# A three-part decoder layer on one core: the scores of all sixteen heads of a batch in one burst, and buffers by planned slot

## The chip, the cores and the metric

The kernel runs on one core of a Trainium2 chip. The metric is the device time of one execution in microseconds; lower is better. Engine names follow the profile: PE (TensorE, matrix products), PEld (its weight loads), DVE (VectorE), ACT (ScalarE), POOL (GpSimd), SP (SyncE, which issues DMAs).

## The reference

One pre-norm decoder layer on x of shape 8 x 112 x 512 in float32:

```python
x = x + attn(layernorm(x))            # 16 heads of 32, RoPE on q and k, causal, biases on q, k, v and the output
x = x + xattn(layernorm(x), ctx)      # q from x; k and v from ctx (375 x 128) by one expansion; causal over (query, key)
x = x + ffn(layernorm(x))             # fp8 products: gelu(x Wg0) * (x Wg1), then Wlin; hidden size 2048
```

Softmax is over the keys, `scores / sqrt(32)`. In cross-attention the causal mask lets query t see context rows 0 to t only, so only 112 of the 375 context rows take part. Each of the two attentions is thus, for each batch and head, a 112 x 112 score matrix with a head size of 32.

## The kernel before

The kernel is written as operations on a planner. `plan.op(eng, cost, fn, r, w, ...)` records one operation with its engine (or a choice of two), an estimated cost, and the buffers that it reads and writes. `Plan.order()` then simulates the engines once, in Python, and fixes the order in which every engine's instructions are issued; on the chip each engine runs its own list in that order and waits on semaphores. Nothing is decided on the chip. Priorities are a longest path (`rank`) and a due time (`plan.at` with the offsets `OFF`, weighted by `BETA`); `SLACK` says how far apart two start times may lie and still be ranked by priority. `CAPS` limits how many buffers of each role are in use.

Tokens: 896 = 7 tiles of 128 (`NT`), but attention works on batches of S = 112. Activations that feed products are held transposed, features on partitions, as a high and a low part (`fm`), and the projections are three products each (`mm3`, line 418: high x high, high x low, low x high).

The steps that matter here:

- `rope_evac` (lines 450 to 462): ACT takes q or k out of PSUM with its bias (`qr`), two SP DMAs swap neighbours (`qs`), DVE or POOL multiply by cos and sin (459, 460) and add (462) into `q` or `k`. It is done by group of four batches (`QG`) and by chunk `m` of four heads.
- `values` (lines 537, 539): v is projected by token tile into `vt` and moved by SP DMAs into `v_sb`, by batch.
- `attention(kind, b)`: for each batch, heads come in four chunks `c` of four heads. Scores (line 479) are taken in bursts of `PAIR` chunks: a head is a 32-row operand, and the four heads of a chunk use the four 32-row tiles of the array at once (mode "row"). Row tile r writes PSUM bank `banks[r]`, so that a burst takes four banks of role `s` (`CAPS["s"]` is 4), and chunk j of the burst takes columns j*112 to (j+1)*112. In the trace each float32 score product is two matmul records.
- For each chunk and head: DVE scales, masks and takes the minimum of the negated scores (line 489, tile `P`), ACT takes the exponential with its sum (492). For each chunk DVE takes the reciprocal (495), POOL or DVE multiplies (496), PE transposes the four 112 x 112 blocks (503, bank `pt`), and ACT or DVE copies them to `pts` (382).
- AV (line 513), when all four chunks are ready: 16 heads, each writing 32 columns of the array (mode "col"), into bank `av`; ACT and DVE split it into `fm` (386, 387).
- `out_proj` (418, 526), `layernorm` (370 to 375, 402 or 400), `cross_kv`, `cross_q`, and `ffn` (646, 653 to 656, 670, 676).

The planner charges a cost `ENTER` when PE changes between ordinary products ("full"), row tiles and column tiles; before the change the transposes count as "full".

Buffers: all eight PSUM banks are one pool with one tag, and all twelve 512-wide temporaries in SBUF (`tmp`: weight staging, `xn`, `qr`, `qs`, `vt`, `P`, `pts` and others) are one tag `t` with twelve buffers. The plan counts how many are free, by role. Which physical buffer a new tile gets is decided by turn in the order of allocation: the one that was allocated longest ago. The tile framework makes the first writer wait until that buffer's last reader is done.

## Time and profile before

| | |
|---|---|
| median of 3 runs | 301.65 us (300.61 to 302.99) |
| the profiled execution | 301.63 us, of which 299.8 us from the first to the last instruction (the span) |
| mean granted TensorE clock | 0.993 |
| score records (line 479) | 512, in 32 bursts of 16; PE busy 22.8 us |
| transposes of P (line 503) | 256; PE busy 36.0 us |
| AV records (line 513) | 512, in 16 bursts of 32; PE busy 15.8 us |
| DVE mask and minimum (line 489) | 256; busy 53.8 us, mean 267 ns |
| ACT exponential (line 492) | 256; busy 96.4 us, mean 382 ns, and 49.2 us of reading the sums, which overlap the next one |

How to read it: busy time of an engine is the union of its instructions. Neighbouring matmuls overlap in the records, since their ends are modelled; the time that one holds PE is read from its start to the start of the next. Self-attention lies between 41 us (first scores) and 142 us (last AV at 140.8), cross-attention between 152 and 226, and from there to 296 only the feed-forward part is left.

### The profile page before, as it was taken

How to read it: one execution, taken by the hardware profiler on the slowest of the kernel's cores; microseconds unless marked ns; L12 is line 12 of the kernel's file. 1: busy time of each engine (PE TensorE's matmuls, PEld its weight loads, DVE VectorE, ACT ScalarE, POOL GpSimd, SP SyncE). 2: the span in 40 equal slices, each digit the busy share in tenths (PEclk: the TensorE clock that was granted, in tenths of full speed). 3: DMA queues.
4: the chain of work that ended last, by engine and by line, in shares of the span. 5: the costliest groups of instructions: out<-in, count | busy, mean ns of one | idle time of the engine just before them, and what ended most of it. 6: DMA issues, size and time to landing. Idle time of an engine off the chain costs nothing.

```text
span 299.8 us, 7577 instructions
## 1 busy us (share of the span) xinstructions
PE 285.9 (95%) x2656; PEld 227.9 (76%) x2656; DVE 228.9 (76%) x909; ACT 203.4 (68%) x710; POOL 108.8 (36%) x111
## 2 busy tenths in 40 slices
PE   7799999896999999999999999999999999999995
PEld 2589877695677777778999987778787577776884
DVE  3798899596599899979559889999967546544564
ACT  4444564358389799999079989999857546545552
POOL 4881518915406478345411442353310101010010
PEclk9999999999899999999999999999999999999999
DMA  7955550301023412207999400000000001010011
GB/s 227 319 176 174 199 192 32 128 32 62 33 68 108 136 43 73 66 3 72 109 104 103 41 2 1 3 2 3 1 2 0 3 0 72 0 37 36 2 72 35
DMA packets 14790, 20.78 MB, mean 69 GB/s; under 512 B 3232, under 2 KB 7584, under 8 KB 14752
## 3 DMA queue, kind: packets, MB, share of 16 engines
q1 hardware_dynamic: 11632, 17.15, 17.5%
q0 software_dynamic: 3120, 3.15, 11.4%
q8 instruction: 21, 0.34, 0.5%
q14 instruction: 17, 0.14, 0.2%
HBM read 22.39 MB, written 1.84 MB: 81 GB/s over the span
## 4 chain that ended last, share of the span: by engine, by line
PE 63%; DVE 3%; ACT 2%; POOL 0%; issue 0%
PE psm L418 22%; PE psfg L646 16%; PE psfo L670 8%; PE pspt L503 7%; PE pss L479 4%; PE psav L513 4%; ACT P L492 1%; PE psm L402 1%; DVE P L489 1%; PE psm L400 1%; DVE pts L382 1%; DVE xnx L375 1%; POOL wxqwl L346 0%; DVE P L496 0%; DVE vt L537 0%
## 5 line engine op out<-in xcount | busy, mean ns | idle before, releaser
L492 ACT ACTIVATE P<-P,at 112x112 f32<-112x112 f32 x256 | 96.4, 382 | 17.4 <-DVE at L489 17.3
L489 DVE CUSTOM_DVE_ANT_0 P<-pss,mask 112x112 f32<-112x112 f32 x256 | 53.8, 267 | 10.4 <-POOL k L462 3.2
L496 POOL TENSOR_TENSOR P<-P,at 112x448 f32<-112x448 f32 x41 | 39.5, 963 | 57.9 <-DVE at L495 29.9
L492 ACT ACTIVATION_READ_ACCUMULATOR P<-P,at 112x1 f32 x256 | 49.2, 192 | 0.0
L503 PE MATMUL pspt<-ident,P 112*112 112x112 f32 x256 | 36.0, 263 | 0.3 <-DVE P L496 0.3
L503 PEld LDWEIGHTS pspt<-ident,P 112*112 112x112 f32 x256 | 27.3, 133 | 8.4 <-issue 2.2
L646 PE MATMUL psfg<-x,wgwh 128*128 128x256 fp8e4 (+1 forms) x256 | 29.1, 259 | 0.0
L646 PE MATMUL psfg<-x,wgwl 128*128 128x256 fp8e4 (+1 forms) x256 | 29.1, 259 | 0.0
L655 DVE TENSOR_TENSOR fb<-gb,fb 128x512 bf16<-128x512 bf16 x28 | 11.5, 421 | 19.1 <-ACT fb L382 17.0
L382 ACT COPY pts<-pspt 112x448 f32<-112x448 f32 x36 | 19.1, 529 | 10.1 <-PE pspt L503 6.3
L646 PEld LDWEIGHTS <-wgwl 128*128 128x128 fp8e4 x256 | 22.4, 98 | 4.4 <-issue 0.3
L479 PE MATMUL pss<-k,q 32*112 32x112 f32 x512 | 22.8, 285 | 2.1 <-DVE at L489 1.4
L646 PEld LDWEIGHTS <-wgwh 128*128 128x128 fp8e4 x256 | 22.2, 98 | 2.9 <-issue 0.7
L479 PEld LDWEIGHTS pss<-k,q 32*112 32x112 f32 x512 | 16.8, 175 | 9.3 <-DVE at L489 2.5
L676 POOL TENSOR_TENSOR x_sb<-x_sb,ob 128x512 f32<-128x512 f32 x3 | 3.5, 1154 | 51.4 <-ACT ob L382 51.4
L489 DVE DVE_READ_ACCUMULATOR2_ANT at<- 112x1 f32 x256 | 21.0, 82 | 0.0
L382 DVE COPY pts<-pspt 112x448 f32<-112x448 f32 x28 | 17.3, 616 | 2.9 <-POOL wxqwl L346 1.3
L565 POOL TENSOR_TENSOR x_sb<-x_sb,bo_t 128x512 f32<-128x512 f32 x7 | 14.5, 2089 | 9.8 <-DMA bo_t<-in_bo_dram 9.8
L653 ACT ACTIVATE gb<-gb 128x512 bf16<-128x512 bf16 x28 | 17.2, 633 | 0.5
L386 ACT CAST fmh<-psm 128x512 fp32r<-128x512 f32 x14 | 8.0, 587 | 12.8 <-PE psm L402 12.8
L496 DVE TENSOR_TENSOR P<-P,at 112x448 f32<-112x448 f32 x23 | 16.1, 705 | 0.4
L382 ACT CAST fb<-psfg 128x512 bf16<-128x512 f32 x14 | 8.3, 590 | 11.9 <-PE psfg L646 11.6
(138 smaller groups left out, 721.8 us busy)
## 6 DMA issues: line engine op xcount, KB each, us to landing
qs<-qr SPq DMA_DIRECT2D x32, 112.0 KB, 2.0
x_sb<-in_x_dram SPq DMA_DIRECT2D x7, 256.0 KB, 4.4
out_dram<-x_sb SPq DMA_DIRECT2D x6, 256.0 KB, 2.0
wst<-in_Wv_dram SPq DMA_DIRECT2D x4, 256.0 KB, 4.3
wst<-in_Wq_dram SPq DMA_DIRECT2D x4, 256.0 KB, 3.5
wst<-in_Wk_dram SPq DMA_DIRECT2D x4, 256.0 KB, 4.2
wst<-in_Wo_dram SPq DMA_DIRECT2D x4, 256.0 KB, 3.2
wst<-in_xWqT_dram SPq DMA_DIRECT2D x4, 256.0 KB, 3.0
```

Source lines behind the costliest of these rows:

```text
L382: lambda e: A.copy(dst(), src()) if e == "act" else V.tensor_copy(dst(), src()), r=r, w=w)
L418: T.matmul(out=out(), lhsT=l(a), rhs=r(b), start=(j == 0 and q == 0), stop=(j == tot - 1 and q == 2))
L479: T.matmul(out=banks[r]()[:S, j * S : (j + 1) * S], lhsT=qk[0]()[rs, c, t0 : t0 + S], rhs=qk[1]()[rs, c, t0 : t0 + S], start=True, stop=True)
L489: op("dve", 0.194, lambda ps=ps, r=r, j=j, Pv=Pv, sm=sm: V.tensor_tensor_reduce(Pv()[:, r, :], ps()[:S, j * S : (j + 1) * S], mask(), -SCA ...
L492: op("act", 0.373, lambda r=r, Pv=Pv, sm=sm: A.activation(Pv()[:, r, :], Pv()[:, r, :], AF.Exp, bias=sm()[:S, r : r + 1], scale=-1.0, accu ...
L496: op(("pool", "dve"), (0.935, 0.535), lambda e, sm=sm, Pv=Pv: LO[e][0].tensor_tensor(Pv(), Pv(), sm()[:S, 8:12].unsqueeze(2).broadcast_to( ...
L503: T.transpose(pt()[:S, r * S : (r + 1) * S], Pv()[:, r, :], ident()[:S, :S])
L513: T.matmul(out=av()[r * 32 : (r + 1) * 32, c * S : (c + 1) * S], lhsT=v_sb()[:, b, h * 32 : (h + 1) * 32], rhs=pts()[:S, r * S : (r + 1) * ...
L565: op("pool", 1.225, lambda i=i: G.tensor_tensor(x_sb()[:, i, :], x_sb()[:, i, :], bo_t(), ALU.add), r=[bo_t], w=[(x_sb, i)], lock=BOTH)
L646: T.matmul(out=ps()[:, j * n : (j + 1) * n], lhsT=wg()[i][:, c, (m + j) * 128 : (m + j + 1) * 128], rhs=x8()[:, c, t0:t1], start=(c == 0), ...
L653: op("act", 0.105 + w / 1200, lambda gb=gb: A.activation(gb()[:, :w], gb()[:, :w], AF.Gelu_apprx_tanh), w=[gb], tab="gelu")
L670: T.matmul(out=ps()[:, :wd], lhsT=a8()[:, m, s], rhs=wl()[0][:, m, hs], start=(m == 0), stop=(m == NH - 1))
```

## The change

`PAIR` goes from 2 to 4: one burst per batch makes the scores of all sixteen heads, 16 products in 32 records, in the same four banks, now with 4 x 112 of their 512 columns in use. The plan's cost for entering a mode now depends on the mode left as well, and transposes have a mode of their own, "tr". The buffers: the plan remembers for each buffer which slot of its role it took, and each slot becomes a tag of its own with a single buffer, so that a tile gets the slot that the plan picked. The planner's constants (`SLACK`, `BETA`, `PAD`, `PADL`, `OFF`) are others, and a few costs differ; the order on every engine is computed anew from these. No instruction is added to or removed from the kernel's work apart from that: the products, transposes and vector operations are the same in number.

```diff
-PAIR = 2
+PAIR = 4
...
         self.tags, self.make, self.ap, self.turn = tags, make, None, {}
+        self.slot = None
...
-            self.ap = self.make()
+            self.ap = self.make(self.slot)
...
-    ENTER = {"full": 0.17, "row": 0.19, "col": 0.13}
+    ENTER = {
+        "full": {"row": 0.27, "col": 0.27, "tr": 0.02}, "tr": {"row": 0.165, "col": 0.165},
+        "row": {"full": 0.095, "tr": 0.095, "col": 0.165}, "col": {"full": 0.095, "tr": 0.095, "row": 0.165},
+    }
...
-        slots = {t: [(0.0, None)] * c for t, c in self.caps.items()}
+        slots = {t: [(0.0, None, k) for k in range(c)] for t, c in self.caps.items()}
...
                     if e == "pe" and o.mode != mode:
-                        late, at = at + MODE, at + self.ENTER[o.mode]
+                        late, at = at + MODE * ("tr" not in (o.mode, mode)), at + self.ENTER[o.mode].get(mode, 0.0)
                     elif e == "pe" and at > f + 0.05:
                         at += 0.09
                     key = (max(late, f + SLACK.get(e, 0.0)), -(o.rank + o.prio), o.n)
...
                         o.after.append(slots[t][k][1])
+                        b.slot = (b.slot or {}) | {t: slots[t][k][2]}
...
-                        slots[t].append((end + 0.2, o))
+                        slots[t].append((end + 0.2, o, b.slot[t]))
...
-SLACK = {'pool': 0.0, 'dve': 0.016728493955868652, 'pe': 0.0, 'sp': 4.441491789066645, 'act': 0.0667493910742207}
-SWITCH, BETA, PAD, PADL, MODE = 20.0, 7.557163650189596, 1.0312597848408145, 1.1187956159584096, 0.0
+SLACK = {'pool': 1.1509329884673878, 'dve': 0.0, 'pe': 0.14620811115369542, 'sp': 3.3963357599814703, 'act': 0.07133249620527977}
+SWITCH, BETA, PAD, PADL, MODE = 20.0, 12.77588534500499, 1.038936327633465, 1.2783297992029616, 0.0
...
     def bank(role):
-        return Buf(("p", role), lambda: psum.tile([128, 512], F32, tag="p", name=nm("ps" + role)))
+        return Buf(("p", role), lambda k: psum.tile([128, 512], F32, tag=f"p{k['p']}", name=nm("ps" + role), bufs=1))
...
     def tmp(name, dt=F32, extra=()):
-        return Buf(("t", *extra), lambda: sb.tile([128, 512], dt, tag="t", name=nm(name), bufs=CAPS["t"]))
+        return Buf(("t", *extra), lambda k: sb.tile([128, 512], dt, tag=f"t{k['t']}", name=nm(name)))
...
-        op("pool", 0.4, lambda: G.tensor_tensor(c(1), c(0), mhalf(), ALU.pow), r=[sm, mhalf], w=[sm], lock=BOTH)
+        op("pool", 0.5, lambda: G.tensor_tensor(c(1), c(0), mhalf(), ALU.pow), r=[sm, mhalf], w=[sm], lock=BOTH)
...
-            op("pe", 0.187 * PAIR, scores, r=[k for c in cs for d in qk for k in K(d, t0, t0 + S, c)], w=banks,
+            op("pe", 0.19 * PAIR, scores, r=[k for c in cs for d in qk for k in K(d, t0, t0 + S, c)], w=banks,
                cols=224 * PAIR, mode="row")
...
-                op("pe", 0.384 + 0.06, tr, r=[*((P, r) for r in range(4)), ident], w=[pt], cols=448)
+                op("pe", 0.384, tr, r=[*((P, r) for r in range(4)), ident], w=[pt], cols=448, mode="tr")
```

The transposes in `layernorm` get `mode="tr"` too, the small buffers (`half`, `sbuf`) get a tag by slot as `tmp` does, and the offsets in `OFF` all change (for example "qk" from -1322.28 to -1337.29, "a" from -2834.99 to -2582.67, "bo" from 684.86 to 1217.33).

## The prediction, made before the result was known

> **What bounds the kernel now.** I read the page's engine line first, then busy time by stage, then the order on TensorE (PE) at its change points, then the waits.

> ```profile
> PE 285.9 (95%) x2656; PEld 227.9 (76%) x2656; DVE 228.9 (76%) x909; ACT 203.4 (68%) x710; POOL 108.8 (36%) x111
> 41.00:60.00 19.00, 16.60 (x107) 13.71 (x106) 15.06 (x50) 9.67 (x34) 14.93 (x8) 1.00 0.27 94
> 60.00:94.00 34.00, 31.11 (x281) 24.19 (x282) 26.45 (x123) 22.78 (x96) 13.06 (x13) 0.95 0.16 51
> 94.00:142.00 48.00, 46.93 (x527) 36.70 (x528) 44.36 (x220) 45.44 (x188) 26.42 (x28) 1.00 0.32 72
> 142.00:152.00 10.00, 10.00 (x59) 9.39 (x58) 5.32 (x13) 2.45 (x6) 3.49 (x5) 1.00 1.06 108
> 152.00:226.00 74.00, 74.00 (x907) 61.14 (x909) 66.17 (x362) 63.81 (x288) 24.71 (x28) 1.00 0.25 24
> 226.00:296.00 70.00, 70.00 (x620) 53.60 (x608) 39.24 (x88) 39.98 (x70) 5.03 (x5) 1.00 0.07 24
> ```

> The first line is the page's; the others are stretches (columns: length, then busy PE, PEld, DVE, ACT, POOL, then clock, DMA share, GB/s). The reader is to see that from 142 us to the end PE has no gap at all, and from 94 to 142 it lacks 1.1 us. 41 to 94 is different: there PE is idle for 5.3 us and its clock falls to 0.95. While attention runs (94 to 142 and 152 to 226), DVE and ACT are close behind, at 86 to 95%. So time is PE work plus PE's early gaps, with two engines near enough to take over.

> **Part 1: one burst of scores in place of two.** PE's timeline shows what a burst costs in its place:

> ```profile
> 162.24 0.28 PE L418 MATMUL psm<-fmh,wxqwl 128*128 128x256 f32 x1
> 162.45 0.66 PE L479 MATMUL pss<-k,q 32*112 32x112 f32 x16
> 163.04 0.59 PE L503 MATMUL pspt<-ident,P 112*112 112x112 f32 x4
> 163.41 0.36 PE L418 MATMUL psm<-fmh,wxqwh 128*128 128x256 f32 x1
> ...
> 165.56 0.59 PE L503 MATMUL pspt<-ident,P 112*112 112x112 f32 x4
> 166.08 0.66 PE L479 MATMUL pss<-k,q 32*112 32x112 f32 x16
> 166.67 0.39 PE L418 MATMUL psm<-fmh,wxqwh 128*128 128x256 f32 x1
> ```

> Read starts, not durations (ends overlap). A burst holds PE 0.59 us (162.45 to 163.04): four rounds of four records, one per 32-row tile. Narrow windows on the same burst show its rounds beginning at 162.45, 162.65 and 162.74: 0.2 us to get going, then 0.10 per round, and about 0.19 from the last round to the next operation. The neighbours pay too. A projection step of 0.12 us takes 0.21 before a burst (+0.09). Four transposes take 0.317 between projections, 0.365 after a burst (+0.05) and 0.478 before one (+0.16). So a whole burst costs 0.59 + 0.16 + 0.02 = 0.77 between transposes and projection (18 of the 32), 0.73 between projection and transposes, 0.79 between projections. Inside a longer burst, the same eight score products are four more rounds: 0.39. AV, 32 records in one burst at 0.905 us, is the nearest row for a burst of 32; 0.59 + 0.39 = 0.98 agrees within 0.08. Each burst absorbed saves 0.34 to 0.40, say 0.37. There are 8 batches in self- and 8 in cross-attention: 16 x 0.37 = **5.9 us less PE work** (5.4 to 6.3).

> How much of it reaches the end? Twelve of the sixteen lie after 94 us, where PE has no gap to lose it in: 4.4 us. Four lie before that, where the next stall can eat it: 0.7 of 1.5. Taken: **-5.1**.

> [...]

> **Part 2: AV next to the scores.** Now mostly AV, transposes, burst (165.56, above). Directly joined, AV and burst would spare about 0.18 (the transposes' 0.16 back to nothing and the 0.02 behind). The one joined pair in the trace, at 68.16 and 68.75, shows 0.59 and 0.91: the join itself adds nothing. Up to 15 junctions: 0 to -2.7. But MODE is 0.0, and `key`, by which the plan picks PE's next operation, uses `late`, into which only MODE goes; ENTER moves only the plan's own times. So the pairs meet by chance: **-0.7**.

> **Part 3: buffers as picked.** The two large early PE stalls come out of buffer turns:

> ```profile
> 59.85 1.22 PE L479 MATMUL pss<-k,q 32*112 32x112 f32 x16 [1.43 <-DVE at L489]
> 73.22 0.59 PE L418 MATMUL psm<-wvwh,fmh 128*128 128x512 f32 x1 [2.31 <-DVE at L489]
> ...
> 59.51 0.28 DVE L489 CUSTOM_DVE_ANT_0 P<-pss,mask 112x112 f32<-112x112 f32 x1 [3.14 <-DMA v_sb<-vt]
> 72.88 0.27 DVE L489 CUSTOM_DVE_ANT_0 P<-pss,mask 112x112 f32<-112x112 f32 x1 [2.44 <-POOL k L462]
> ```

> DVE's softmax step has its scores, yet waits for a DMA that reads `vt` and for POOL's rope sum: neither makes anything it needs; they were the last readers of the `t` buffer whose turn it was. Behind it the score banks stay full, and PE waits. At 73.22 PE wants a bank for values and gets, by turn, one that still holds scores. Cost: 1.43 + 2.31; then six projections 0.43 apart at half clock instead of 0.23 (+1.2) and the burst at 59.85 lasting 1.15 instead of 0.59 (+0.56): 5.5 us. With the planned slot there is no wait the plan doesn't know of; but the plan may know these, having only 12 slots. Between 0 and -5.5, I take **-2.5**. The new tags and slot bookkeeping issue no instruction.

> **Part 4: what a burst now waits for.** It needs q and k of all four chunks. Now the first burst starts at 41.40 and the second, which needs the other chunks, at 52.45, when DVE ends the last rope sums (50.85 to 52.53). Queued behind the burst on PE is whatever the plan puts there; DVE's 8 softmax steps and ACT's 8 exponentials (of 0.375 start to start) come later with it. DVE's work is only exchanged with rope work; ACT loses up to 3.0 us of early work, in a stage where it is idle 39% of the time. Between 0 and +11.05 (the full delay), I take **+1.5**, the nearest cover being ACT's idle time. In steady running no new wait: a burst still needs all four score banks, and the `P` tiles are still four, so the wait for the oldest `P` still comes one chunk after the banks are free. The new order constants, POOL's 0.5 in place of 0.4 for the layernorm power and the new SLACK only redraw the order; no row prices that, and it widens the range by 3 either way.

> **Sum.** 299.8 - 5.1 - 0.7 - 2.5 + 1.5 = 293.0 span. The profiled execution took 301.63 around it (+1.8), the median is 301.65: **294.8 us**. Less than 1% (3 us) can't be told from no change.

> **Rivals.**

> *Evacuation takes over*: PE's saving turns into PE gaps, DVE and ACT hold the 8.5 us per batch. [...] For it: 95% ACT from 94 to 142. Against: idle ACT time of 7.5 us from 142 to 152, and feed-forward products that already fill PE from 200 on.

> *The late first burst decides* (slower): the exponentials start 11.05 us later. From 94 on, DVE and ACT at 92 to 95% can't catch up, PE runs out of projections (the last of the values now begins near 92) and waits. Then 301.6 + 11.05 - 5.9 = 306.8. It decides once the last AV of self-attention comes over 7 us later than now (140.8). Against: 39% idle ACT time before 94, and a PE that today reaches the cross stage with 10 us of its own work in hand.

> *Larger gain*: all early stalls go and the pairs join: 301.6 - 5.9 - 2.7 - 5.5 = 287.5.

> *The change doesn't do what it says*: the burst stalls inside, since its banks come free and its chunks come ready one by one. The first burst now, which waits inside for a q sum, takes 1.5 us (41.40 to 42.93) in place of 0.59; a wait of 0.37 in each of 16 cancels part 1: about 300. Held within the first rival.

> **How the numbers follow.** Forecast (289.5 to 298.6): 0.52. Evacuation, or stalls inside bursts: 0.13. Late burst or an order as bad: 0.23. Larger gain: 0.12. Faster is the first plus the last: 0.64; same 0.13; slower 0.23. The range drops a tenth on each side: 288 to 305; the forecast's own range is 289.5 to 298.6.

> **What would show it.** L479: 16 bursts of 32 records, each 0.90 to 0.98 us to the next start. PE busy near 279, idle near 13. `P L489` no longer waiting for `vt` or rope sums. DVE and ACT still below PE from 152 to 226. First burst near 50. It is wrong if PE shows new gaps after 94 us, if the last self-attention AV is past 148, or if the burst's start-to-start is over 1.2 us.

## The result, and the profile after

The changed kernel takes 304.77 us (median of 9 runs, 303.21 to 309.23); the kernel before, measured along with it, 302.45. The ratio is 1.0082 (95% interval 1.0053 to 1.0111): a little slower, where 294.8 was forecast. Executions more than 1.5% above the fastest of their kernel are left out of the ratios here and below, but not of the medians. The profiled execution has a span of 302.8 us. Only the mean PE clock tells at once that something has happened: 0.977, against 0.993 before.

Page of the kernel after, span and engine line:

```profile
span 302.8 us, 7575 instructions
PE 285.4 (94%) x2656; PEld 231.1 (76%) x2656; DVE 229.6 (76%) x914; ACT 202.4 (67%) x703; POOL 103.1 (34%) x113
```

PE is busy 285.4 us, hardly less than the 285.9 before; 279 was expected. Its timeline around a burst (line numbers of `attention` are five higher after the change: scores 484, mask 494, transposes 508):

```profile
107.31 0.59 PE L508 MATMUL pspt<-ident,P 112*112 112x112 f32 x4
107.83 1.05 PE L484 MATMUL pss<-k,q 32*112 32x112 f32 x32
108.82 0.50 PE L423 MATMUL psm<-wowh,fmh 128*128 128x512 f32 x1
```

From start to start the burst of 32 holds PE for 0.99 us, in place of two that took 0.59 and their neighbours' extra. There are 16 of these, 13 of them at 0.98 to 0.99; the saving is there. Some stretches show what has swallowed it (columns: from and to, length, busy PE, PEld, DVE, ACT, POOL, clock, DMA share, GB/s):

```profile
41.00:60.00 19.00, 17.27 (x130) 15.11 (x130) 17.14 (x60) 10.05 (x39) 3.36 (x3) 0.91 0.34 117
60.00:94.00 34.00, 30.48 (x290) 23.98 (x289) 26.21 (x125) 24.27 (x104) 15.71 (x15) 0.95 0.18 59
94.00:102.00 8.00, 5.35 (x45) 4.38 (x44) 3.62 (x22) 3.19 (x16) 1.87 (x2) 0.79 0.13 36
102.00:142.00 40.00, 40.00 (x442) 32.75 (x444) 37.93 (x190) 35.84 (x147) 22.70 (x25) 1.00 0.21 61
172.00:185.00 13.00, 11.00 (x106) 8.65 (x105) 9.43 (x54) 9.06 (x42) 6.16 (x7) 0.87 0.68 68
185.00:228.00 43.00, 43.00 (x550) 34.56 (x549) 40.25 (x204) 38.21 (x165) 18.09 (x22) 1.00 0.01 2
```

Wherever PE has gaps in these rows the clock falls too: 0.91, 0.95, 0.79 and 0.87. Stretch by stretch, 1 - clock times the length is 1.7 us. That is four windows of 3.4 us at half clock (granted clock 0.50 from 54.1, 84.8, 98.4 and 180.4 us on, 1.00 in the rest of the span), a loss of up to 6.8 us of PE time, where before there was one (0.51 from 73.4 to 76.9 us). PE's timeline has a gap ahead of each window; in brackets stand its length and what ended it:

```profile
52.83 0.46 PE L484 MATMUL pss<-k,q 32*112 32x112 f32 x8 [1.73 <-DVE k L467]
...
83.57 1.52 PE L484 MATMUL pss<-k,q 32*112 32x112 f32 x32 [1.70 <-DVE at L494]
85.02 0.79 PE L423 MATMUL psm<-wvwh,fmh 128*128 128x512 f32 x1
85.61 0.63 PE L423 MATMUL psm<-wvwl,fmh 128*128 128x512 f32 x1
...
97.97 2.18 PE L484 MATMUL pss<-k,q 32*112 32x112 f32 x30 [2.65 <-DVE at L494]
...
179.47 0.47 PE L423 MATMUL psm<-ch,wkvh 128*128 128x448 f32 x1 [1.26 <-ACT ch L591]
```

In the two gaps near 82 and 95 a burst waits for the masking step, because its banks are still full. The first of these bursts then holds PE 1.45 us instead of 0.98, though the clock is full until 84.8: four masking steps, 0.20 us apart from 83.23 on, free its banks one by one. Behind it, at half clock, the first projection step takes 0.59 us (85.02 to 85.61); behind the burst above it takes 0.34 (108.82 to 109.16). The chain of waits in the window 79 to 101 us goes on from there (start, length, what):

```profile
79.39 0.43 SPq L544
79.87 3.23 DMA v_sb<-vt
83.23 0.28 DVE P L494
83.57 1.52 PE pss L484 x32
...
90.13 2.37 DMA v_sb<-vt
92.62 0.09 DVE vt L542
...
93.90 3.58 DMA v_sb<-vt
97.64 0.27 DVE P L494
97.97 2.18 PE pss L484 x30
```

Masking needs nothing of `vt`. It waits for the DMA that reads `vt` since its `P` tile has been given that memory. The plan's slots put it there: `order()` frees a slot at `end + 0.2`, and for a DMA `end` is when SP has issued it. The plan counts the landing for those who read what the DMA writes, but not for the buffer that it reads. Here SP's issue took 0.43 us and the DMA another 2.4 to 3.6, so for about 3 us `vt`'s slot counts as free in the plan while the DMA is still reading it, and can be picked as the earliest one.

### The profile page after: what moved, and what is told of

It reads as the page before. It is cut to its first block, busy times and chain, and to the rows that moved or that the text cites. A ratio compares the mean times of both kernels' runs of the same rounds, so it can differ in the third digit from the quotient of the medians.

```text
span 302.8 us, 7575 instructions
## 1 busy us (share of the span) xinstructions
PE 285.4 (94%) x2656; PEld 231.1 (76%) x2656; DVE 229.6 (76%) x914; ACT 202.4 (67%) x703; POOL 103.1 (34%) x113
## 4 chain that ended last, share of the span: by engine, by line
PE 80%; DMA 8%; DVE 6%; issue 2%; ACT 1%; SPq 1%; POOL 1%; DVEq 0%; ACTq 0%; POOLq 0%
PE psm L423 37%; PE psfg L651 16%; PE psfo L675 8%; PE pspt L508 8%; PE pss L484 5%; PE psav L518 4%; DMA v_sb<-vt 3%; DMA cst<-in_ctxT_dram 3%; DMA x_sb<-in_x_dram 2%; PE psm L407 2%; DVE P L494 1%; DVE qr L464 1%; SPq L320 1%; DVE pts L387 1%; DMA qs<-qr 1%
## 5 line engine op out<-in xcount | busy, mean ns | idle before, releaser
L501 POOL TENSOR_TENSOR P<-P,at 112x448 f32<-112x448 f32 x48 | 45.1, 944 | 71.7 <-DVE at L500 48.6
L508 PE MATMUL pspt<-ident,P 112*112 112x112 f32 x256 | 37.1, 268 | 0.7 <-ACT pts L387 0.7
L508 PEld LDWEIGHTS pspt<-ident,P 112*112 112x112 f32 x256 | 28.4, 136 | 8.4 <-issue 1.9
L387 DVE COPY pts<-pspt 112x448 f32<-112x448 f32 x35 | 21.7, 620 | 6.7 <-PE pspt L508 6.0
L660 DVE TENSOR_TENSOR fb<-gb,fb 128x512 bf16<-128x512 bf16 x28 | 11.6, 422 | 17.6 <-ACT fb L387 15.3
L484 PE MATMUL pss<-k,q 32*112 32x112 f32 x512 | 19.2, 276 | 6.1 <-DVE at L494 4.4
L387 ACT COPY pts<-pspt 112x448 f32<-112x448 f32 x29 | 15.4, 531 | 7.8 <-PE pspt L508 7.5
L387 ACT CAST fb<-psfg 128x512 bf16<-128x512 f32 x16 | 9.4, 587 | 12.3 <-PE psfg L651 12.1
L518 PE MATMUL psav<-pts,v_sb 112*32 112x112 f32 x512 | 15.6, 262 | 0.8 <-ACT pts L387 0.8
L518 PEld LDWEIGHTS psav<-pts,v_sb 112*32 112x32 f32 x512 | 11.7, 109 | 5.7 <-ACT pts L387 1.6
L423 PE MATMUL psm<-fmh,wxqwh 128*128 128x256 f32 (+1 forms) x48 | 15.3, 319 | 0.0
```

What stands on the lines that cost most here:

```text
L387: lambda e: A.copy(dst(), src()) if e == "act" else V.tensor_copy(dst(), src()), r=r, w=w)
L423: T.matmul(out=out(), lhsT=l(a), rhs=r(b), start=(j == 0 and q == 0), stop=(j == tot - 1 and q == 2))
L484: T.matmul(out=banks[r]()[:S, j * S : (j + 1) * S], lhsT=qk[0]()[rs, c, t0 : t0 + S], rhs=qk[1]()[rs, c, t0 : t0 + S], start=True, stop=True)
L501: op(("pool", "dve"), (0.935, 0.535), lambda e, sm=sm, Pv=Pv: LO[e][0].tensor_tensor(Pv(), Pv(), sm()[:S, 8:12].unsqueeze(2).broadcast_to( ...
L508: T.transpose(pt()[:S, r * S : (r + 1) * S], Pv()[:, r, :], ident()[:S, :S])
L518: T.matmul(out=av()[r * 32 : (r + 1) * 32, c * S : (c + 1) * S], lhsT=v_sb()[:, b, h * 32 : (h + 1) * 32], rhs=pts()[:S, r * S : (r + 1) * ...
```

## The experiments

All of them compute the whole layer. Ratios are to the kernel before, run beside each on the same chip.

| kernel | what it is (`vt` in memory of its own: see a_vtown) | median us | ratio (95%) |
|---|---|---|---|
| after | the change | 304.77 | 1.0082 (1.0053 to 1.0111) |
| a_vtown | after's order, `vt` in memory of its own | 293.27 | 0.9685 (0.966 to 0.971) |
| a_rot | after's order, buffers by turn | 294.54 | 0.9721 (0.9695 to 0.9746) |
| b_slot | before's order, planned slots | 301.3 | 0.993 (0.9903 to 0.9958) |
| a_split | after, each burst split by a mode change | 306.15 | 1.0104 (1.0064 to 1.0145) |
| v_split | a_vtown, each burst split | 297.69 | 0.9818 (0.9771 to 0.9866) |
| b_vtown | b_slot, `vt` in memory of its own | 297.01 | 0.9803 (0.9755 to 0.9851) |
| a_dma | after, slot free at the DMA's landing | 296.17 | 0.9749 (0.9704 to 0.9795) |
| v_pair2 | a_vtown with `PAIR = 2` | 312.36 | 1.0275 (1.0202 to 1.0347) |
| a_warm | after, two gaps filled with products of zeros | 302.21 | 0.9952 (0.9926 to 0.9978) |
| r_vtown | a_rot, `vt` in memory of its own | 296.7 | 0.975 (0.9704 to 0.9795) |
| dv_11 | version with the causes mended | 294.82 | 0.9703 (0.9661 to 0.9745) |
| dv_13 | the same, other constants | 292.63 | 0.9646 (0.9612 to 0.9681) |

**Take away what makes P wait: a_vtown.** The order on every engine stays; the two `vt` tiles move into `a8`, which lies idle until the feed-forward part.

```diff
-        vt = tmp("vt", extra=("vt",))
+        vt = Buf(("t", "vt"), lambda k: a8()[:, k["vt"] * 4 : k["vt"] * 4 + 4, :].bitcast(F32).rearrange("p a b -> p (a b)"))
```

> The kernel after, with its whole issue order unchanged; only the two value tiles vt lie in memory of their own (in a8, idle until the feed-forward part), so that no P tile takes over a buffer that a vt DMA still reads. Theory 1 (P waits for vt's DMA, PE stalls behind it, and its clock halves): the DVE waits of 2.65 and 3.79 us on v_sb<-vt go, with them the PE gaps of 1.7 and 2.65 us near 82 and 95 and one or two of the four half-clock windows (1.7 us each): 297 to 301 us, clock above 0.98. Theory 2 (DVE and ACT set the pace, the saved PE time has nowhere to go): the same 304 to 305. Theory 3 (the new order is worse as such): 303 to 305.

Measured: 0.9685 (293.27 us), faster than theory 1's 297 to 301. Page of a_vtown, span and engine line:

```profile
span 291.2 us, 7559 instructions
PE 277.9 (95%) x2656; PEld 225.0 (77%) x2656; DVE 228.2 (78%) x914; ACT 201.6 (69%) x703; POOL 103.8 (36%) x113
```

Its stretch for the first half of self-attention (columns as above):

```profile
60.00:94.00 34.00, 31.95 (x335) 24.92 (x334) 31.87 (x160) 28.55 (x126) 18.85 (x18) 1.00 0.21 67
```

The clock stays at 1.00, and from 60 to 94 us DVE does 31.87 us of work where it did 26.21. Against the kernel after, the span is 11.6 us shorter: 4.1 of idle PE time (17.4 to 13.3) and 7.5 of busy PE time (285.4 to 277.9), of which the four half-clock windows account for up to 6.8. By this count the two waits on `vt` stand for their two gaps and two of the windows, some 7.8 us (1.70 + 2.65 + 2 x 1.7, an estimate). The other two windows, up to 3.4 us, went as well, and that was not foreseen: the gaps ahead of them are shorter here (1.36 us at 52 and 0.99 at 168). Theories 2 and 3 (DVE and ACT set the pace; the order as such is worse) fall: with the same order and the same evacuation the kernel is 3.2% faster than before.

**Buffers by turn in the new order: a_rot.**

```diff
-        return Buf(("t", *extra), lambda k: sb.tile([128, 512], dt, tag=f"t{k['t']}", name=nm(name)))
+        return Buf(("t", *extra), lambda k: sb.tile([128, 512], dt, tag="t", name=nm(name), bufs=CAPS["t"]))
```

The PSUM banks, `half` and `sbuf` likewise.

> The kernel after with the same order on every engine, but buffers by turn as before the change. The prediction's part 3 (planned slots spare waits): slower by 1 to 5 us, 306 to 310, with more DVE waits at the masking step. Theory 1 (a planned slot hands P the vt buffer whose DMA the plan does not count): within 2 us of 304.8 either way, the vt waits replaced by other ones.

Both theories missed: 0.9721, some 11 us faster than the kernel after (1.0082). The waits of masking in a_rot that are left (us in total, times, longest):

```profile
DVE P L494 <- POOL wxqwl L351: 1.2, 1, 1.2
DVE P L494 <- PE pss L484: 0.7, 2, 0.5
DVE P L494 <- POOL P L501: 0.5, 1, 0.5
DVE P L494 <- PE psav L518: 0.2, 1, 0.2
```

None is on `vt`. By turn, `P` gets the buffer allocated longest ago. The plan picks the one that it believes free first, which can be just the one whose DMA has been issued. So the slots alone cost the kernel after about 3.6% of its time.

**Planned slots in the old order: b_slot.** The reverse edit on the kernel before.

> The kernel before with the same order on every engine, only its buffers by planned slot. The prediction's part 3: 2.5 us faster (0 to 5.5), the DVE waits on v_sb<-vt and on the rope sum at the masking step gone. Theory 1: the plan frees vt's slot at the DMA's issue, so a P tile still lands on it: 0 to 1.5 us faster at most.

Measured 0.993 (0.9903 to 0.9958): about 2 us faster, near the 2.5 of the prediction, but not in the way that was predicted. Its masking waits:

```profile
DVE P L491 <- DMA v_sb<-vt: 6.3, 2, 3.5
DVE P L491 <- PE pss L481: 1.6, 5, 0.7
DVE P L491 <- PE pspt L505: 1.0, 1, 1.0
```

The wait on the rope sum (3.2 us before) is gone, and the one on `vt` has doubled, from 3.1 us before to 6.3.

**Planned slots in the old order, without the DMA wait: b_vtown.** b_slot with the edit of a_vtown.

> The kernel before in its own order, with planned slots and vt in memory of its own: the change's buffers alone, without the wait that they brought. Theory 1: b_slot's two waits on v_sb<-vt (6.3 us of DVE) and its two half-clock windows go, 296 to 299. If the wait matters only in the after order: 301 as b_slot.

As theory 1 said: 0.9803. Page of b_vtown, span and engine line:

```profile
span 294.9 us, 7559 instructions
PE 283.3 (96%) x2656; PEld 226.3 (77%) x2656; DVE 235.0 (80%) x909; ACT 203.2 (69%) x710; POOL 104.7 (36%) x111
```

At nearly full clock (1.000 and 0.997), PE is busy 283.3 us here and 277.9 in a_vtown. The burst and the order together are worth 5.4 us of PE work, and in time the step from 0.9803 to 0.9685, 1.2% or 3.6 us.

**Is PE's work what the time is made of? a_split and v_split.** The burst is split where it was two, by one tiny full-array product into columns that nothing reads:

```diff
                 for j, c in enumerate(cs):
+                    if j == 2:
+                        T.matmul(out=banks[0]()[:, 448:452], lhsT=zero()[:, :128], rhs=zero()[:, :4], start=True, stop=True)
                     for r in range(4):
```

> The kernel after with the same order, but between chunks 1 and 2 of each burst one tiny full-array product (4 columns of zeros, into unused columns of the burst's first bank), so that PE changes its tiling twice more per batch, as two bursts did. The price of a split is about 0.40 us each, 16 of them 6.4 us. Prediction's part 1 (PE work passes to the end): slower by 4 to 7 us, 309 to 312. Theory 2 (DVE and ACT set the pace): slower by less than 1.5 us.

In the kernel after the answer stayed open: 1.0104 against 1.0082, with overlapping intervals, where 309 to 312 us was expected of part 1. PE is busy 288.8 us, 3.4 more, and the span is the same. The clock hides part of the cost: 0.977 to 0.989 over these runs, 0.972 to 0.978 over those of after, and the profile has three half-clock windows in place of four, 1.7 us less lost. So the same was done where there are no such gaps.

> a_vtown (293.3 us, the after order with vt in memory of its own) with the tiny full-array product between chunks 1 and 2 of each burst, in the same order. Without the large stalls PE sets the pace, so the split should now show in full: 16 x 0.40 = 6.4 us, 298 to 300.5. If DVE and ACT set the pace (theory 2), the cost hides: below 295.

```profile
span 295.3 us, 7593 instructions
PE 283.2 (96%) x2672; PEld 228.1 (77%) x2672; DVE 230.6 (78%) x914; ACT 201.8 (68%) x703; POOL 103.2 (35%) x113
```

Page of v_split: PE's busy time grows from 277.9 to 283.2, 0.33 us for each split, and the time by 4.4 us by the medians (297.69 against 293.27), which come from two sessions, or 4.0 by the ratios (0.0133 of 303). That is just under the expected 298 and far from hidden: three quarters or more of PE's added work reach the end.

**One line in the plan: a_dma.**

```diff
-                        slots[t].append((end + 0.2, o, b.slot[t]))
+                        slots[t].append((max(end + 0.2, dma + 0.9 if o.mb else 0.0), o, b.slot[t]))
```

> The kernel after with one line of the plan changed: a buffer that a DMA reads comes free when the DMA is expected to land, not 0.2 us after its issue. The order is drawn anew. Theory 1: the plan no longer gives P a vt buffer in flight, so the waits on v_sb<-vt fall below 2 us and the time comes near a_vtown, 292 to 297. If the order as such is at fault, or the estimate of the landing too short: 300 to 305.

0.9749, within the expected 292 to 297, and no masking step waits for `vt` (its waits there: 2.0 us on the scores, 0.3 on a layernorm product). This mends the cause in the plan itself; the order differs from after's, so it does not isolate the wait as a_vtown does.

**What the half clock costs beside the gap: a_warm.** Before the two bursts that stall, PE gets products of zeros to do (the lines that keep `last_av` are left out):

```diff
...
             def scores(banks=banks, cs=cs):
+                for _ in range({3: 28, 4: 44}.get(b, 0) if kind == "a" else 0):
+                    T.matmul(out=last_av[b - 2]()[:, 448:512], lhsT=zero()[:, :128], rhs=zero()[:, :64], start=True, stop=True)
```

> The kernel after with its order, plus products of zeros on PE (28 ahead of the self-attention burst of batch 3, 44 ahead of that of batch 4, each 64 columns, into unused columns of an AV bank), which fill the two gaps in which PE waits for the masking steps behind vt's DMA. The waits themselves stay. If the half clock that follows such a gap is a cost of its own, the half-clock windows after them go and the kernel gains up to 2 x 1.7 us: 301 to 303, clock about 0.99. If the clock's dip costs nothing beside the wait: 304.8 or, by the added products, up to 1 us more.

0.9952 against 1.0082 for after: adding work to PE makes the kernel 1.3% faster, about 4 us, a little over the 3.4 expected. The waits on `vt` are still there (5.6 us, 6.4 in after). The clock over the runs goes from 0.972 to 0.978 up to a median of 0.989. PE's timeline in a_warm, at the first gap:

```profile
81.23 0.98 PE L486 MATMUL psav<-zero 128*128 128x64 bf16 x28
83.22 1.43 PE L490 MATMUL pss<-k,q 32*112 32x112 f32 x32 [1.02 <-DVE at L500]
84.58 0.50 PE L423 MATMUL psm<-wvwh,fmh 128*128 128x512 f32 x1
84.92 0.39 PE L423 MATMUL psm<-wvwl,fmh 128*128 128x512 f32 x1
85.15 0.40 PE L423 MATMUL psm<-wvwh,fml 128*128 128x512 f32 x1
```

The gap is now 1.02 us instead of 1.70, and the projections behind it start 0.34 and 0.23 apart, not 0.59. The profile has full clock from 83 to 104 us, so both windows behind the `vt` waits are gone. It is one of a_warm's longest executions (304.58 us, clock 0.981): one window at 52 has stayed, and two from 178.5 to 185.3 follow a gap of 2.25 us in cross-attention that this edit does not touch. So the clock is a cost of its own; its size is read from the 22 runs, not from this one.

**PAIR alone: v_pair2.** `PAIR = 2` in a_vtown.

> a_vtown with PAIR back at 2, everything else (constants, entering costs, slots, vt of its own) as in it; the order is drawn anew with constants that were not chosen for it. The merged burst alone is worth 5.9 us of PE work: 299 us if the rest of the order holds, up to 308 with the loss of an unsuited order; below 296 would say that the burst was not where the gain came from.

Missed on the slow side: 1.0275, some 18 us behind a_vtown. The order is drawn anew from constants that weren't chosen for it, so this cannot be read as the price of two bursts (v_split puts that at 4 us). That the rest comes from the unsuited order is likely, but no run shows by which step.

**Are planned slots worth having? r_vtown.** a_rot with the edit of a_vtown.

> The kernel after in its own order, with buffers by turn as in a_rot and vt in memory of its own as in a_vtown. It tells what planned slots are worth once no P tile can meet a vt DMA. If slots still spare waits: slower than a_vtown (293.3) by about 1 us or more. If the only thing that the choice of buffers did was to put P on vt: 293 to 294.

0.975 (0.9704 to 0.9795) against 0.9685 (0.966 to 0.971) with slots: about 2 us in favour of slots, the intervals just touching. The clock alone may explain it: the median is 0.988 in r_vtown and 0.994 in a_vtown, 1.8 us of lost clock, and the one run of each at a clock of 1.0 took 293.38 and 293.18 us. So what planned slots are worth once the wait is away stays open. The intervals of a_rot and r_vtown overlap, which agrees with a_rot's waits: by turn there was no `vt` wait to lose.

**A version that beats both: dv_11 and dv_13.** Bursts of all four chunks, planned slots, a_dma's line, and `vt` in `a8` and no longer counted among the `t` buffers; the planner's constants picked anew for this.

> A candidate for a version that beats both: bursts of four chunks, planned slots, vt in memory of its own and no longer counted among the t buffers, a buffer that a DMA reads comes free at the DMA's landing, and the planner's constants picked anew for that. PE work is that of a_vtown (278 us busy), so 290 to 293 if its gaps stay as they are there; up to 297 if the redrawn order brings early stalls.

> As dv_11 with another set of constants, from another search: 290 to 294, up to 297 with early stalls.

dv_13 is at 0.9646, 3.5% under the kernel before and 4.3% under the change (0.9646/1.0082); dv_11 at 0.9703. Against a_vtown the intervals overlap, so the new constants aren't shown to add anything.

## Why the prediction was wrong

Of the four steps of the sum, the first held, the second and fourth were not measured by themselves, and the third had the wrong sign in the kernel as built.

- **Part 1 was right.** 0.98 us was worked out for a burst of 32, and 0.98 to 0.99 came out. The saving was put at 5.9 us of PE work (5.4 to 6.3): b_vtown to a_vtown, order included, is 5.4, v_split 5.3. The share that passes on was put at 5.1 of 5.9; the runs give 4.0 to 4.4 of 5.3 and 3.6 of 5.4, so a little too much was counted. By the first rival, in which DVE and ACT take over, the split would have been free; v_split shows 4.0 to 4.4 us.
- **Part 2** was small and stays small: one AV stands directly ahead of a burst, among fifteen places. No run measured what that is worth.
- **Part 3 failed**: "With the planned slot there is no wait the plan doesn't know of". It took -2.5 out of 0 to -5.5, and allowed for no loss. The plan doesn't know when a DMA has finished reading a buffer, and by picking the slot that it thinks free first it finds that very slot. In after's order slots cost 11 us (a_rot). The row was in the prediction: a masking step that waited 3.14 us for `v_sb<-vt`. I put it down to turns, and didn't ask what the plan's own release time for that slot was, though the line `end + 0.2` stood in the diff. The 2.5 us that part 3 hoped for are not shown: b_slot gains 2 us with the `vt` wait doubled, and r_vtown against a_vtown, the wait taken out, differs by no more than its clock.
- **The clock** was priced for a stall that was to go (+1.2 in part 3; the +0.56 there is a burst that waits at full clock), never for stalls to be gained. Four windows instead of one: up to 6.8 us in place of 1.7. The prediction's own sign of being wrong, new PE gaps after 94 us, came: 2.65 us at 98 and 1.26 at 179.
- **Part 4** foretold a first burst near 50 us, and it came at 50.2, with a gap of 1.7 us inside. Like the gap near 82 it carries a half-clock window. a_vtown has the same late burst, at 50.2, with a gap of 1.36, and keeps its clock. The slower rival, the late burst deciding, is refuted: the last AV of self-attention is at 141.3, against 140.8, and a_vtown shares the late burst and is the fast one.

The forecast of 294.8 is thus what the change gives with either buffer rule that avoids the wait (294.5 by turn, 293.3 with `vt` apart). That it meets these numbers is partly luck: by turn the sum has no part 3, and without it comes to 297.3. The gain that was expected was there, and was given back to DMA waits of 6.4 us on DVE, which PE turned into gaps and half clock. What made the fourth half-clock window, in cross-attention near 180, is read only from the trace: PE waits 1.26 and 0.74 us for the context's split, behind a DMA of the context that took 8.25 us. It wasn't tried by itself; a_vtown, which shares its order, has two gaps there as well (0.99 and 0.74) and no dip.

## What to carry to other kernels

When a planner chooses buffers, its release time must be the end of the last read, and for a DMA that is the landing (for `vt` 2.4 to 3.6 us behind its issue); a choice of "free first" seeks out the mistake where turns would mostly miss it. In a kernel paced by PE, price a new gap at its length plus the half-clock window that it may bring (here up to 1.7 us behind gaps of 1.26 to 2.65 us). And when a change both removes work and alters waiting, vary the waiting in the same issue order: two such runs (after and a_vtown) separated here a gain of 3% from a loss of 4%.

## What the runs showed of the hardware

The lost clock goes with much of the scatter between runs. Over 62 runs of the kernel before, taken with the experiments, its span rises by 0.68 us for each microsecond of clock lost ((1 - clock) x span), with a correlation of clock and span of -0.80: 302.7 us on average at 0.981 (10 runs) and 300.5 at 0.993 (8 runs).
